# A vision-Mamba chain: the image convolution of three layers divided over four engines

## The chip, the cores and the metric

The kernel runs on one core of one Trainium2 chip. The metric is the device time of the whole program in microseconds (us), as the median of repeated executions. TensorE, VectorE, ScalarE, GpSimd and SyncE appear in the profile as PE (with PEld for its weight loads), DVE, ACT, POOL and SP. All data is float32.

## The reference

Eight images of 64 x 64 positions and 96 channels pass through four layers. Each layer adds to `x` what a selective-scan block makes of the group-normalized `x`. Cut to what matters here (layer 0; layers 1 and 2 differ in the order in which positions are walked, layer 3 has one direction and a causal convolution of three taps in its place):

```python
xz = gn(x) @ in_proj_w.T                      # 96 channels -> 2 * 192
xpart, z = split(xz, 2)
xc = depthwise_conv_3x3(xpart, conv_w)        # 192 channels, 9 taps each, SAME padding
xc = silu(xc + conv_b)
xs = [xc by rows, xc by columns, both reversed]              # K = 4 directions
dts, Bs, Cs = split(einsum(xs, x_proj_w))
delta = softplus(einsum(dts, dt_proj_w) + dt_proj_b)
for t in positions:                           # for each channel and 16 states
    h = exp(delta[t] * A) * h + delta[t] * u[t] * B[t]
    y[t] = sum_over_states(h * C[t])
y = layernorm(sum over directions of (y + D * u)) * silu(z)
x = x + y @ out_proj_w.T
```

## The kernel before

**Loops.** A hardware loop runs over the eight images. In its body the four layers stand one after the other, and within a layer the stages follow each other: normalization, convolution, scans, output. The 192 inner channels are held as a half 0 of 128 partitions and a half 1 of 64; the 4096 positions are eight chunks of 512, that is of eight image rows.

**Normalization.** DVE takes the statistics (L211), ACT forms `scale` with Ln and Exp (L227, L228), DVE forms `shift` (L230) and writes the normalized image `xn` with a border of zeros, chunk by chunk (L247).

**Convolution (L248 to L317).** The input projection and the nine taps are folded into one set of weights: `taps` is the tap times the projection (L197), and PE sums nine matmuls over shifted views of `xn` into one PSUM tile (L270). This makes 12 units: eight chunks of half 0, and four pairs of chunks of half 1, whose two chunks share one tile of 128 partitions. ACT applies SiLU with the bias (L290; L283 and L286 in layer 1, where even and odd columns go to different places) and a DMA stores the rows as `u_mem[0]` (L291, L297). The column order `u_mem[1]` is made by strided copies of DVE and GpSimd (L312 to L315) and stored (L316). In this stage the order on each engine is chosen by the framework's scheduler.

**Scans (`scans`).** 32 chunks are walked (eight in layer 3), 24 scan steps each. This part's order is written out by hand: a `plan` says in which of the 24 slots of a chunk each preparing step of the next chunk is issued, on PE, DVE, ACT and POOL in order. The steps that the text names:

- `scan` (L664, DVE): one recurrence of 128 x 512; its decay is made by `decay` four steps ahead (L650, ACT, Exp, six buffers), its input by `enter` (L633, PE, two PSUM buffers).
- `turn_v` (L521, PE) makes the delta projection and the B columns; `keep_b` (L551, ACT) keeps the latter.
- `softplus` (ACT): Abs (L542), Exp (L544), Ln (L546), twice a chunk, followed by `delta_of` (L556, DVE), `turn_back` (L607, PE) and `keep_delta` (L612, L616, ACT). The Ln of the first half stands in slot 6, that of the second in slot 13.
- `neg_a` (L764 on ACT, L765 on DVE) is made once a layer, before the first scan.
- `diagonal` (L577, POOL) and `diagonals` (L590, ACT) spread B; `keep` (L678, ACT) keeps states; `read_out` (L682, POOL) multiplies by C; `add_up` (L696, PE) sums over states; `close_sums` (L718 to L724, DVE) adds to the outputs.

**Activation tables.** Exp, Ln and SiLU need tables loaded into ACT. The kernel names the set itself, once for a stage, through `tables` (L108 to L112), and asks that the stage's instructions on ACT be issued after that load:

```python
load = tc.keep_in_program_order(tc.nc.scalar.preload_act_table_set(name))
with tc.issue_after(load.ins):
    yield
```

The convolution's set is `silu_and_others`; that of normalization and scans is `natural_log_exp_and_others`. Where the order that results leaves ACT with a set that lacks the next function, the build puts a load in front of that instruction.

Of the kernel before, what the change touches and what calls it, by code (L numbers as in the profile page):

```python
# [22 lines left out]
F32 = mybir.dt.float32  # L23
AF = mybir.ActivationFunctionType
ALU = mybir.AluOpType
# [3 lines left out]
NB, H, W, C = 8, 64, 64, 96  # L29
L = H * W  # L30
DI = 192
# [4 lines left out]
CH = 512  # L36
NCH = L // CH
# [8 lines left out]
class Layer:  # L46


    def __init__(self, dirs, rank, order, taps, norm):
        self.dirs, self.rank, self.order, self.taps, self.norm = dirs, rank, order, taps, norm  # L50

        self.x_rows = 33 + rank if dirs == 1 else 64 + 33 + rank
        at = 0
        for name, n in (
            ("win_x", DI),
            ("win_z", DI),
            ("x_proj", min(dirs, 2) * 2 * self.x_rows),
            ("dt_w", dirs * (DI + NS)),
            ("a_log", dirs * NT * NJ),
            ("d", dirs * 2),  # L60
            ("conv_b", 2),
            ("gamma", 2),
            ("beta", 2),
            ("w_out", 2 * C),
        ):
            setattr(self, name, at)
            at += n
        self.width = at
# [38 lines left out]
@contextmanager  # L107
def tables(tc, name):  # L108
# [55 lines left out]
def layer(tc, env, x, x_of, x_to, n, ly):  # L164

    nc = tc.nc
    const, small, big = env.const, env.small, env.big
# [6 lines left out]
    def mm(name):  # L174
        return env.ps_m.tile([128, CH], F32, tag="mm", name=name)
# [8 lines left out]
    def piece(name):  # L184
# [2 lines left out]

    w = env.wts.tile([128, W_MAX], F32, tag="w", name=f"w{n}")[:, : ly.width]
    nc.sync.dma_start(w, env.packs[n])
    taps = env.cpool.tile([C, 9 * DI], F32, tag="c", name=f"taps{n}")  # L190
    taps = taps[:, : ly.taps * DI].rearrange("p (t d) -> p t d", d=DI)
    nc.sync.dma_start(
        taps.rearrange("p t d -> p (t d)"), env.convs[n].partition_broadcast(C)
    )
# [30 lines left out]
    scale = small.tile([C, 1], F32, name="scale")  # L225
# [4 lines left out]
    nc.vector.scalar_tensor_tensor(shift, mean, -1.0, scale, ALU.mult, ALU.mult)  # L230


    image = ly.taps == 9
# [7 lines left out]
    for c in range(NCH):  # L241
        if image:
            to = xn[:, 1 + 8 * c : 9 + 8 * c, 1 : W + 1]
            of = chunk(c).rearrange("p (h w) -> p h w", w=W)
        else:
            to, of = xn[:, 2 + c * CH : 2 + (c + 1) * CH], chunk(c)
        nc.vector.tensor_scalar(to, of, scale, shift, ALU.mult, ALU.add)  # L247
    u_mem = [env.dram.tile([DI, L], F32, tag=f"u{o}", name=f"u{o}_{n}") for o in range(min(K, 2))]  # L248
    serpentine = ly.order == "serpentine"
    with tables(tc, "silu_and_others"):  # L250
        for half, (d0, nd) in enumerate(((0, 128), (128, 64))):

            u0 = [env.hpool.tile([128, L // 2], F32, tag="h", name="u0") for _ in range(2)]
            rows = [
                u0[c // 4][0:nd, c % 4 * CH : c % 4 * CH + CH].rearrange("p (h w) -> p h w", w=W)
                for c in range(NCH)
            ]

            for c0 in range(NCH if half == 0 else NCH // 2):
                both = (c0,) if half == 0 else (c0, c0 + NCH // 2)  # L260
                p = mm("conv")
                parts = [p[64 * o : 64 * o + nd] for o in range(len(both))]
                for t in range(ly.taps):
                    for c, part in zip(both, parts):
                        if image:
                            rhs = xn[:, 8 * c + t // 3 : 8 * c + t // 3 + 8, t % 3 : t % 3 + W]
                            out = part.rearrange("p (h w) -> p h w", w=W)
                        else:
                            rhs, out = xn[:, c * CH + t : (c + 1) * CH + t], part
                        nc.tensor.matmul(  # L270
                            out,
                            taps[:, t, d0 : d0 + nd],
                            rhs,
                            start=t == 0,
                            stop=t == ly.taps - 1,
                        )
                for o, (c, part) in enumerate(zip(both, parts)):
                    bias = w[64 * o : 64 * o + nd, ly.conv_b + half : ly.conv_b + half + 1]
                    got = part.rearrange("p (h w) -> p h w", w=W)
                    if serpentine:  # L280

                        even, odd = slice(0, W, 2), slice(1, W, 2)
                        nc.scalar.activation(  # L283
                            rows[c][:, :, even], got[:, :, even], AF.Silu, bias=bias
                        )
                        nc.scalar.activation(  # L286
                            rows[NCH - 1 - c][:, ::-1, odd], got[:, :, odd], AF.Silu, bias=bias
                        )
                    else:
                        nc.scalar.activation(rows[c], got, AF.Silu, bias=bias)  # L290
                        nc.sync.dma_start(  # L291
                            u_mem[0][d0 : d0 + nd, c * CH : (c + 1) * CH],
                            rows[c].rearrange("p h w -> p (h w)"),
                        )
            if serpentine:
                for r in range(2):
                    nc.sync.dma_start(  # L297
                        u_mem[0][d0 : d0 + nd, r * L // 2 : (r + 1) * L // 2], u0[r][0:nd]
                    )
            if K > 1:  # L300
                for v in range(2):
                    u1 = env.diags.tile([128, L // 2], F32, tag="diag", name="u1")
                    to = u1[0:nd].rearrange("p (w h) -> p w h", h=H)
                    for r in range(2):
                        of = u0[r][0:nd].rearrange("p (h w) -> p w h", w=W)
                        engine = nc.vector if r == 0 else nc.gpsimd
                        here = slice(32 * v, 32 * v + 32)
                        if serpentine:

                            there = slice(63 - 32 * v, 31 - 32 * v if v == 0 else None, -1)  # L310
                            up, down = slice(32 * r, 32 * r + 32, 2), slice(32 * r + 1, 32 * r + 32, 2)
                            engine.tensor_copy(to[:, :, up], of[:, here, 0::2])  # L312
                            engine.tensor_copy(to[:, :, down], of[:, there, 1::2])
                        else:
                            engine.tensor_copy(to[:, :, 32 * r : 32 * r + 32], of[:, here, :])  # L315
                    nc.sync.dma_start(  # L316
                        u_mem[1][d0 : d0 + nd, v * L // 2 : (v + 1) * L // 2], u1[0:nd]  # L317
                    )


    y_a = big.tile([128, L], F32, tag="big0", name="y_a")
# [3 lines left out]


    chunks = [slice(c * CH, (c + 1) * CH) for c in range(NCH)]
    halves = [slice(0, 64), slice(64, 128)]

    def single(o, name):  # L330
        return env.ps_y.tile([128, CH], F32, tag=f"y{o}", name=name)
# [474 lines left out]
    return a  # L806


def pack(ly, win, conv_b, x_proj, dt_w, dt_b, a_log, d, w_out, gamma=None, beta=None):
    K, R = ly.dirs, ly.rank  # L810
    XP = 33 + R
    a = np.zeros((128, ly.width), np.float32)
# [21 lines left out]
    d = d.reshape(K, DI)  # L834
    a[:, ly.d : ly.d + K] = d[:, :128].T
    a[0:64, ly.d + K : ly.d + 2 * K] = d[:, 128:].T
    for v, at in ((conv_b, ly.conv_b), (gamma, ly.gamma), (beta, ly.beta)):
# [17 lines left out]
def layouts(inputs):  # L855
    arrays = {"x": inputs["x"].reshape(-1, L, C).transpose(0, 2, 1), "const": constants()}
    for n, (ly, (pre, names)) in enumerate(zip(LAYERS, _NAMES)):
        arrays[f"pack{n}"] = pack(ly, *(inputs[pre + s] for s in names.split()))
# [23 lines left out]
```

## Time and profile before

| | |
|---|---|
| median of 3 runs | 33116.64 us (33102.38 to 33124.26) |
| profiled execution, its own time | 33112.82 us |
| its span in the profile | 33108.9 us |
| granted TensorE clock | 0.979 |
| DVE, ACT and POOL busy | 27562.6, 25739.6, 26418.0 us |
| folded-tap matmuls of the convolutions (L270) | 2580.0 us |
| table loads on ACT (L110) | 152, 1283 ns each |

Durations of single instructions come from the profiled execution. In a row of the profile, "out<-in" gives the tiles' names and "xcount | busy, mean ns of one | idle" how often, for how long, how long one takes, and how long its engine had stood idle before it. Instructions of one engine overlap a little, so the distance between the starts of two is less than the duration of one.

### The profile page before, as it was taken

The page shows a single profiled execution, that of the slowest core. Times are in us where ns is not written, and L with a number is a line of the kernel's source. Part 1 is how long each engine was busy: PE and PEld are TensorE (multiplying, and loading weights), DVE is VectorE, ACT ScalarE, POOL GpSimd, SP SyncE. Part 2 cuts the span into 40 slices and gives each one's busy share as a digit, 9 for nine tenths or more (in the row PEclk, how much of TensorE's full clock was granted, in tenths as well). Part 3 has the DMA queues.
Part 4 walks back from the last instruction along what each step waited for, and adds up shares of the span by engine and source line. Part 5 has one row for each costly group of instructions (what it writes and reads, how often), then busy time and mean ns, then how long its engine had stood idle before and what let it go on. Part 6 is the DMA issues. An engine that isn't in the chain of part 4 may idle for free.

```text
span 33108.9 us, 958242 instructions
## 1 busy us (share of the span) xinstructions
PE 32013.2 (97%) x406784; PEld 17321.5 (52%) x406784; DVE 27562.6 (83%) x28224; ACT 25739.6 (78%) x65112; POOL 26418.0 (80%) x8764
## 2 busy tenths in 40 slices
PE   9999999999999999999999999999999999999999
PEld 5555555555555555555555555555555455555555
DVE  8798887988879788798887988879888798887988
ACT  7787777877778777787777877778777787777877
POOL 7797777977779777797777977779777797777977
PEclk9999999999999999999999999999999999999999
DMA  3333333333333333333333333333333333333333
GB/s 84 73 77 80 72 83 73 77 79 72 83 73 78 78 72 84 73 78 78 72 84 73 78 78 72 84 74 77 79 72 84 73 77 78 73 83 74 77 79 72
DMA packets 1232983, 2550.36 MB, mean 77 GB/s; under 512 B 107024, under 2 KB 107024, under 8 KB 1202576
## 3 DMA queue, kind: packets, MB, share of 16 engines
q1 hardware_dynamic: 1228688, 2488.70, 33.6%
q8 instruction: 3232, 52.95, 0.7%
q14 instruction: 1063, 8.71, 0.1%
HBM read 2213.81 MB, written 274.46 MB: 75 GB/s over the span
## 4 chain that ended last, share of the span: by engine, by line


## 5 line engine op out<-in xcount | busy, mean ns | idle before, releaser
L682 POOL TENSOR_TENSOR h<-h,c 128x2048 f32<-128x2048 f32 x4992 | 22716.7, 4555 | 1984.7 <-ACT state L678 923.6
L664 DVE TENSOR_TENSOR_SCAN h<-d_a,state,dbu 128x512 f32<-128x512 f32 x17472 | 21080.0, 1261 | 1142.5 <-PE dbu L633 614.3
L650 ACT ACTIVATE d_a<-delta,neg_a 128x512 f32<-128x512 f32 x19968 | 14188.8, 716 | 45.2 <-DVE h L664 22.6
L633 PE MATMUL dbu<-diag,du_t 64*64 64x128 f32 x319488 | 11176.7, 277 | 228.8 <-DVE h L664 134.0
L633 PEld LDWEIGHTS dbu<-diag,du_t 64*64 64x64 f32 x319488 | 8746.7, 134 | 5025.0 <-issue 4641.1
L696 PE MATMUL y_ps<-h,const 128*64 128x512 f32 x39936 | 10805.5, 617 | 77.8 <-POOL h L682 64.8
L590 ACT ACTIVATE diag<-const,bt 128x64 f32<-128x64 f32 x26624 | 7840.9, 344 | 23.2 <-DMA u<-u 17.0
L577 POOL TENSOR_TENSOR diag<-const,bt 128x512 f32<-128x512 f32 x3328 | 3471.1, 1044 | 547.7 <-ACT bt L551 448.4
L664 DVE TENSOR_TENSOR_SCAN h<-d_a,dbu 128x512 f32<-128x512 f32 x2496 | 2893.4, 1204 | 437.8 <-PE dbu L633 238.2
L696 PEld LDWEIGHTS y_ps<-h,const 128*64 128x64 f32 x39936 | 2061.2, 135 | 1848.2 <-issue 1507.3
L521 PE MATMUL v<-w,x_dbl 39*128 39x208 f32 (+1 forms) x6656 | 2657.7, 483 | 159.5 <-ACT x_dbl L483 103.0
L521 PEld LDWEIGHTS v<-w,x_dbl 39*128 39x128 f32 (+1 forms) x6656 | 1796.9, 317 | 1736.9 <-issue 887.3
L270 PE MATMUL conv<-xn,taps 96*128 96x512 f32 (+1 forms) x7680 | 2580.0, 606 | 115.1 <-issue 69.6
L607 PEld LDWEIGHTS delta_ps<-const,delta_t 128*64 128x64 f32 (+1 forms) x19968 | 1678.8, 158 | 1422.6 <-issue 926.3
L616 ACT COPY delta<-delta_ps 64x512 f32<-64x512 f32 x3328 | 1930.5, 580 | 542.8 <-PE delta_ps L607 496.8
L607 PE MATMUL delta_ps<-const,delta_t 128*64 128x128 f32 (+1 forms) x19968 | 2277.6, 292 | 29.2 <-DVE delta_t L556 29.2
L270 PEld LDWEIGHTS conv<-xn,taps 96*128 96x128 f32 (+1 forms) x7680 | 1029.9, 167 | 1639.7 <-issue 1639.7
L551 ACT COPY bt<-v 128x32 f32<-128x32 f32 x1664 | 303.8, 183 | 1961.1 <-PE v L521 1960.5
L315 POOL COPY u<-u 128x1024 f32<-128x1024 f32 (+1 forms) x64 | 139.9, 2212 | 1736.3 <-ACT u L290 1736.3
L290 ACT ACTIVATE u<-conv,w 128x512 f32<-128x512 f32 (+1 forms) x384 | 263.2, 685 | 1619.1 <-PE conv L270 1481.5
L534 PEld LDWEIGHTS u_t<-const,u 128*128 128x128 f32 x3328 | 650.1, 195 | 1602.7 <-issue 887.6
L678 ACT COPY state<-h 128x4 f32<-128x4 f32 x4992 | 972.2, 195 | 546.5 <-DVE h L664 505.9
(86 smaller groups left out, 15802.0 us busy)
## 6 DMA issues: line engine op xcount, KB each, us to landing
c<-cm SPq DMA_DIRECT2D x1792, 512.0 KB
c<-xm SPq DMA_DIRECT2D x1536, 512.0 KB
u<-u SPq DMA_DIRECT2D x1024, 256.0 KB
u<-u SPq DMA_DIRECT2D x1024, 128.0 KB
u<-u SPq DMA_DIRECT2D x64, 1024.0 KB
x_mem<-x SPq DMA_DIRECT2D x48, 768.0 KB
x<-x_mem SPq DMA_DIRECT2D x48, 768.0 KB
u<-u SPq DMA_DIRECT2D x64, 512.0 KB
```

The costliest lines, as they stand in the source:

```text
L270: nc.tensor.matmul(out, taps[:, t, d0 : d0 + nd], rhs, start=t == 0, stop=t == ly.taps - 1,)
L521: nc.tensor.matmul(turned[i, e, "v"][:, b], block(2 * e + b, dbls[i]), w[0:XP, at : at + DI + NS], start=True, stop=True,)
L577: nc.gpsimd.tensor_tensor(diags[i, 0][:, b], sel.unsqueeze(1).unsqueeze(3).to_broadcast([128, NH, 64, 2]), of.unsqueeze(2).to_broadcast([1 ...
L590: nc.scalar.activation(diags[i, 1][:, b, q // 2, :, q % 2], sel, AF.Copy, scale=turned[i, b // 2, "b"][:, b % 2, NJ + q : NJ + q + 1],)
L607: nc.tensor.matmul(block(b, to), of_, ident, start=True, stop=True)
L616: nc.scalar.copy(delta[64 * half : 64 * half + 64], of)
L633: nc.tensor.matmul(to[64 * half : 64 * half + 64, e, b], du[rows, b, 64 * t : 64 * t + 64], diag[rows, b, 2 * half + pair], start=True, st ...
L650: nc.scalar.activation(d_a, deltas[i, t], AF.Exp, scale=neg_a[:, at : at + 1])
L664: nc.vector.tensor_tensor_scan(hs[s][:, m4, flow], decays.pop(m)[:, flow], p[:, flow], 0.0 if first else states[i // NCH][:, j : j + 1], A ...
L678: nc.scalar.copy(states[i // NCH][:, at : at + NH], hs[s][:, :, last])
L682: nc.gpsimd.tensor_tensor(hs[s], hs[s], cs[i, g], ALU.mult)
L696: nc.tensor.matmul(sums[i][o][64 * half : 64 * half + 64], sel, hs[of][:, state, :], start=g == 0 and e in (0, 4), stop=g == 1 and e in (3 ...
```

## The change

In layers 0 to 2 the convolution is divided. PE folds taps for four of the 12 units alone (chunks 4 to 7 of half 0). For the other eight units PE makes only the input projection (`project`), ACT copies it from PSUM into a bordered tile `xin` (`keep`), and nine scaled, shifted views of `xin` are summed (`by_sums`): on DVE for five units (all four pairs of half 1, and chunk 3 of half 0) into a PSUM tile, and for three units (chunks 0 to 2 of half 0) by ACT, which scales each view, and GpSimd, which adds it. The weight pack gains the taps as columns, and only the 128 folded columns of half 0 are made in layers 0 to 2. Column copies and row stores of both halves now stand after the convolution, half 1 first. Layer 3 keeps the folded form.

The core of the diff (the bodies that only moved into the functions `activate`, `by_taps`, `by_columns`, `by_rows` are left out):

```diff
...
     win_x = w[0:C, ly.win_x : ly.win_x + DI]
     nc.vector.tensor_tensor(
-        taps, taps, win_x.unsqueeze(1).to_broadcast([C, ly.taps, DI]), ALU.mult
+        taps, taps, win_x[:, 0:by_pe].unsqueeze(1).to_broadcast([C, ly.taps, by_pe]), ALU.mult
     )
...
     with tables(tc, "silu_and_others"):
-        for half, (d0, nd) in enumerate(((0, 128), (128, 64))):
...
-            for c0 in range(NCH if half == 0 else NCH // 2):
-                both = (c0,) if half == 0 else (c0, c0 + NCH // 2)
-                p = mm("conv")
...
+        if not image:
+            for c in range(NCH):
+                by_taps(0, (c,))
+            for c in range(NCH // 2):
+                by_taps(1, (c, c + NCH // 2))
+        else:
+            xin = big.tile([128, 2, 34, W + 2], F32, tag="big1", name="xin")
+            nc.gpsimd.memset(xin[:, :, :, 0 :: W + 1], 0.0)
...
+            def project(half, rows_):
+                n_, p = len(rows_[0]), wide("xin")[:, 0:CH]
+                d0, nd = widths[half]
+                for o, r in enumerate(rows_):
+                    nc.tensor.matmul(
+                        as_rows(p[64 * o : 64 * o + nd, 0 : n_ * W]),
+                        win_x[:, d0 : d0 + nd],
+                        xn[:, r[0] + 1 : r[0] + 1 + n_, 1 : W + 1],
+                        start=True,
+                        stop=True,
+                    )
+                return as_rows(p[:, 0 : n_ * W])
+
+            def keep(half, c, p):
+                nc.scalar.copy(xin[:, half, 1 + 8 * c : 9 + 8 * c, 1 : W + 1], p)
+
+            def by_sums(half, c, acc, together=True):
+                for t in range(9):
+                    of = xin[:, half, 8 * c + t // 3 : 8 * c + t // 3 + 8, t % 3 : t % 3 + W]
+                    at = ly.conv_w + 9 * half + t
+                    tap = w[:, at : at + 1]
+                    if not together:
+                        by = acc if t == 0 else piece("by_tap")
+                        nc.scalar.activation(as_rows(by), of, AF.Copy, scale=tap)
+                        if t:
+                            nc.gpsimd.tensor_tensor(acc, acc, by, ALU.add)
+                    elif t == 0:
+                        nc.vector.tensor_scalar(as_rows(acc), of, tap, None, ALU.mult)
+                    else:
+                        nc.vector.scalar_tensor_tensor(
+                            as_rows(acc), of, tap, as_rows(acc), ALU.mult, ALU.add
+                        )
+
+            edge = project(1, (range(32, 33), range(31, 32)))
+            nc.scalar.copy(xin[0:64, 1, 33:34, 1 : W + 1], edge[0:64])
+            nc.scalar.copy(xin[64:128, 1, 0:1, 1 : W + 1], edge[64:128])
+            nc.scalar.copy(xin[:, 0, 33:34, 1 : W + 1], project(0, (range(32, 33),)))
+            for c in range(4):
+                keep(1, c, project(1, (range(8 * c, 8 * c + 8), range(32 + 8 * c, 40 + 8 * c))))
+                keep(0, c, project(0, (range(8 * c, 8 * c + 8),)))
+            for c in range(4):
+                if c < 3:
+                    acc_p = env.decays.tile([128, CH], F32, tag="d_a", name="acc_p")
+                    by_sums(0, c, acc_p, False)
+                    activate(0, c, acc_p)
+                acc = single(c % 2, "acc")
+                by_sums(1, c, acc)
+                for o in range(2):
+                    activate(1, c + 4 * o, acc, o)
+                by_taps(0, (c + 4,))
+            acc = single(0, "acc")
+            by_sums(0, 3, acc)
+            activate(0, 3, acc)
+        for half in (1, 0):
             if serpentine:
-                for r in range(2):
-                    nc.sync.dma_start(
...
+                by_rows(half)
             if K > 1:
...
+                by_columns(half)
```

More of the change, by code (lines that the diff above doesn't have):

```diff
@@ L249, in layer @@
     serpentine = ly.order == "serpentine"
-    with tables(tc, "silu_and_others"):
-        for half, (d0, nd) in enumerate(((0, 128), (128, 64))):
[L253 to L257, printed above, removed]
-            for c0 in range(NCH if half == 0 else NCH // 2):
-                both = (c0,) if half == 0 else (c0, c0 + NCH // 2)
-                p = mm("conv")
[L262 to L275, printed above, removed]
-                        )
[L277 to L294, printed above, removed]
@@ new lines, in by_taps @@
+    def by_taps(half, both):
+        d0, nd = widths[half]
+        p = mm("conv")
+        for t in range(ly.taps):
+            for o, c in enumerate(both):
+                part = p[64 * o : 64 * o + nd]
+                if image:
+                    rhs = xn[:, 8 * c + t // 3 : 8 * c + t // 3 + 8, t % 3 : t % 3 + W]
+                    part = as_rows(part)
+                else:
+                    rhs = xn[:, c * CH + t : (c + 1) * CH + t]
+                nc.tensor.matmul(
+                    part, taps[:, t, d0 : d0 + nd], rhs, start=t == 0, stop=t == ly.taps - 1
+                )
+        for o, c in enumerate(both):
+            activate(half, c, p, o)
@@ new lines, in by_columns @@
+    def by_columns(half):
+        d0, nd = widths[half]
+        for v in range(2):
+            u1 = env.diags.tile([128, L // 2], F32, tag="diag", name="u1")
+            to = u1[0:nd].rearrange("p (w h) -> p w h", h=H)
+            for r in range(2):
+                of = u0[half][r][0:nd].rearrange("p (h w) -> p w h", w=W)
+                engine = nc.vector if r == 0 else nc.gpsimd
+                here = slice(32 * v, 32 * v + 32)
+                if serpentine:
+                    there = slice(63 - 32 * v, 31 - 32 * v if v == 0 else None, -1)
+                    up, down = slice(32 * r, 32 * r + 32, 2), slice(32 * r + 1, 32 * r + 32, 2)
+                    engine.tensor_copy(to[:, :, up], of[:, here, 0::2])
+                    engine.tensor_copy(to[:, :, down], of[:, there, 1::2])
+                else:
+                    engine.tensor_copy(to[:, :, 32 * r : 32 * r + 32], of[:, here, :])
+            nc.sync.dma_start(
+                u_mem[1][d0 : d0 + nd, v * L // 2 : (v + 1) * L // 2], u1[0:nd]
+            )
@@ L836, in pack @@
     a[0:64, ly.d + K : ly.d + 2 * K] = d[:, 128:].T
+    conv_w = conv_w.reshape(DI, ly.taps)
+    a[:, ly.conv_w : ly.conv_w + ly.taps] = conv_w[:128]
+    for p in (0, 64):
+        a[p : p + 64, ly.conv_w + ly.taps : ly.conv_w + 2 * ly.taps] = conv_w[128:]
     for v, at in ((conv_b, ly.conv_b), (gamma, ly.gamma), (beta, ly.beta)):
@@ L857, in layouts @@
     for n, (ly, (pre, names)) in enumerate(zip(LAYERS, _NAMES)):
-        arrays[f"pack{n}"] = pack(ly, *(inputs[pre + s] for s in names.split()))
+        arrays[f"pack{n}"] = pack(
+            ly, inputs[pre + "conv_w"], *(inputs[pre + s] for s in names.split())
+        )
     for n, (ly, (pre, _)) in enumerate(zip(LAYERS, _NAMES)):
```

72 lines of the change are left out of this document (44 added, 28 removed).

## The prediction

> **What bounds the kernel now.** I read the page first, then the stretches of one image, then the waits of a scan stage, last the seams between the stages, in order of time. In a row of stretches the columns are length, then busy time (and instructions) of PE, PEld, DVE, ACT, POOL, the granted clock, the DMA share and GB/s.
>
> ```profile
> 4154.30:4251.90 97.60, 97.60 (x291) 38.97 (x292) 4.32 (x7) 10.92 (x16) 3.90 (x2) 0.97 0.19 66
> 4251.90:4267.40 15.50, 11.71 (x75) 8.18 (x73) 7.35 (x7) 12.00 (x32) 8.92 (x6) 0.67 0.67 149
> 4267.40:5327.60 1060.20, 1048.40 (x15070) 595.55 (x15070) 1000.13 (x954) 931.44 (x2395) 990.48 (x315) 0.99 0.37 80
> ```
>
> These are layer 0 of the second image: convolution, seam, scans. The convolution is PE alone: 97.6 us with the other engines nearly idle. In the scans all four work: PE 99%, DVE 94%, POOL 93%, ACT 88%. There are 24 convolutions (8 images x 3 layers), so 2342 us lie in the first kind of stretch, and 24 x 1060 in the third.
>
> ```profile
> 300.00:1100.00 800.00, 797.54 (x11533) 453.72 (x11531) 762.10 (x729) 713.62 (x1840) 758.76 (x244) 1.00 0.37 81
> ...
> ACT bt L551 <- PE v L521: 55.7, 38, 1.8
> ACT delta L616 <- PE delta_ps L607: 18.6, 20, 1.2
> DVE h L664 <- PE dbu L633: 20.4, 28, 1.6
> ```
>
> Inside the scans of the first image, 800 us hold 24.3 chunks (146 `keep`, six a chunk), 32.9 us each. ACT works 29.4 us of a chunk and waits 3.55, nearly all of it for PE. PE sets the pace; ACT's spare is 3.55 us a chunk.
>
> ```profile
> L718 DVE SCALAR_TENSOR_TENSOR y_a<-u,d,y_ps 128x512 f32<-128x512 f32 x192 | 139.0, 724 | 31.5 <-PE y_ps L696 31.5
> L577 POOL TENSOR_TENSOR diag<-const,bt 128x512 f32<-128x512 f32 x3328 | 3471.1, 1044 | 547.7 <-ACT bt L551 448.4
> L765 DVE TENSOR_SCALAR neg_a<-neg_a 128x96 f32<-128x96 f32 x24 | 54.5, 2272 | 0.0
> L765 DVE TENSOR_SCALAR neg_a<-neg_a 128x24 f32<-128x24 f32 x8 | 1.4, 178 | 271.1 <-ACT neg_a L764 271.1
> L110 ACT ACT_TABLE_LOAD x152 | 195.0, 1283 | 77.2 <-PEq L144 73.6 <-PEq L869 1.1
> ...
> 2629.46 1.39 ACT L290 ACTIVATE u<-conv,w 64x512 f32<-64x512 f32 x2 [6.33 <-PE conv L270]
> 2630.87 1.28 ACT L110 ACT_TABLE_LOAD   x1
> 2632.16 0.28 ACT L764 ACTIVATE neg_a<-w 128x96 f32<-128x96 f32 x1
> ```
>
> The first two rows price a sum on DVE and an add on GpSimd. The last three show what a table load costs ACT: it starts 0.02 us after the last SiLU ended and the next instruction follows 0.01 us after it, 1.30 in all; the overlap of 0.10 that neighbours have (0.72 us decays start 0.62 apart) is lost too: **1.40 us**.
>
> **The convolution stage.** I count t from the end of `shift` (L230) in layer 2 of the first image, 2529.94; there PE begins at 2533.40 and the last SiLU ends at 2630.85, t = 100.9.
>
> - PE loses eight of 12 units of 7.72 us (nine matmuls of 0.858) and gains eight projections of 0.86: 36 x 0.858 + 8 x 0.86 = 37.8. It starts when `xn` chunk 4 is written: two chunks (0.98), 1152 of 1728 folded columns (1.30 of 1.95), three chunks (1.45), t = 3.7. The stretch's 96.0 us against 12 x 7.72 = 92.6 show 3.4 of slow start, which I keep; with the edges 0.5: PE ends at 45.4.
> - DVE gains 45 operations. The nearest row is L718, 0.724 with one PSUM input; dependent DVE operations start 0.03 after the one before: 40 x 0.754 + 5 x 0.54 (L247) = 32.9, from the first copied chunk at 8.5 to 41.4. Two column copies of half 1 stand between, 1.9 each as now beside GpSimd's (L315): 45.2. Bounds: 0.66 an operation (L724) and 1.26 (the scan, same shape), 41 to 65.
> - POOL gains 24 adds of 1.04 (L577; 1.14 as a quarter of L682): 25 us from t = 12, with two hand-overs from ACT of 2: 41.
> - ACT gains eight copies (0.49 apart, L616), three edges (0.25), 27 scalings (0.62 to 0.72) beside its 16 SiLU (0.70): 33 us from t = 4, with waits for all others.
>
> DVE's last sum is latest: its SiLU ends at 45.9. In the built order of layers 0 and 2, ACT then has this (in layer 1 the stage's own load comes after the last SiLU, as before):
>
> ```
> 47 L281 Activation u_166<-acc,w_118 128x512 [waits DVE_49]
> 48 L111 LoadActFuncSet
> 49 L281 LoadActFuncSet
> 50 L281 Activation u_167<-conv,w_118 128x512 [waits PE_49]
> 51 L850 LoadActFuncSet
> 52 L850 Activation neg_a_435<-w_118 128x96
> ```
>
> The last SiLU of a folded unit slipped behind the load of the scans' set. Two loads stand ahead of it: 45.9 + 2.6 + 0.7 = 49.2, **51.7 earlier** than 100.9. In layer 1 without them 46: 55.5 earlier than its 101.5.
>
> **The seam.** After row 51 the set in ACT is no longer the one with both Ln and Exp: the build loads in front of each Ln (L632) and of the first Exp after it. Up to the first decay that is five loads where one was: 4 x 1.30 = 5.2, of which the chain's waits for PE take about 1.2: +4 in layers 0 and 2, which gain 47.7. In layer 1 the first load of `u` waits for the row stores behind the last SiLU, now 2 MB of half 0 where 1 MB of half 1 was: 1 MB at the 178 GB/s of that seam is 6 us; layer 1 gains 49.5. The DVE and GpSimd copies of half 0 run after the last SiLU as those of half 1 did, 4 us. Sum: 16 x 47.7 + 8 x 49.5 = **1159 us saved**.
>
> The column copies and stores of half 0 moved behind the convolution. On SP's queue the two stores of 1 MB, which wait for the copies, stand ahead of the stores of `x_dbl` and the spreading of C, as the two of 0.5 MB of half 1 did; GpSimd's `diagonal` and DVE's `neg_a` stand behind the copies, again as before. The L765 rows show that neighbour: 2.27 us beside GpSimd's copies, 0.18 without. The 40 sums, which read PSUM as the scans do (1.26 us beside a GpSimd that is 93% busy), I leave free of it.
>
> **The scans.** Rows 48 to 52 go on: 64 pairs of loads in each scan stage of layers 0 and 2, four a chunk. The built program has 279 loads an image where 19 were: 2232 executed in place of 152. A chunk's ACT gains 4 x 1.40 = 5.6 us and has 3.55 to spare.
>
> What absorbs it: at slots 6 and 7 two loads put ACT 2.8 late; its wait of 1.76 for `turn_v` in slot 11 goes; at 13 and 14 two more; the wait of 0.9 for `turn_back` goes. What is left, about 2 us a chunk, eats the lead of three to four decays within two chunks; then DVE waits for decays and ACT sets the pace. Does ACT still wait then? DVE, held by ACT, finishes scan 9 before ACT is past decay 13, so PE has `turn_v` done 2 to 3 us before `keep_b`; `turn_back` comes out 2 us early as well. `delta_of` of slot 8 now waits for its Ln, about 1 us, which DVE (31.3 us a chunk) makes good by the chunk's end.
>
> So a scan stage is ACT's work: 933 us (931 to 936 in three layers) less 15 of the last chunk, plus 62 pairs x 2.8 = 174, makes 1092 for 31 chunks; plus 33 for the last, less the lead of 4: 1121, +61. I take +64 for small waits in the chunks that also copy `x_dbl`. The other end is all waits kept: +174. I take the low end since every input of ACT has slack. 16 x 64 = **1024 us lost**.
>
> The Trainium skill (ScalarE: Activation LUTs, What ACT_TABLE_LOAD costs) adds a drain of about 1380 ns to each switch of set. The trace shows none: 0.02 us before the load and 0.01 after. By the page a chunk's ACT would be some 40 us and the kernel about 2600 us slower (an estimate from its 2.66 us a switch). The same page (Table sets) says Exp and Ln share one set and need one load; that speaks against what the build makes of this change.
>
> **Sum.** 33112.8 (the profiled execution's own time, 3.8 under the median of 33116.6) - 1159 + 1024 = **32978 us**. About 0.2%, 66 us, is what a measurement can tell from no change.
>
> **The rivals.**
>
> 1. *ACT's waits stay (slower).* If PE or DVE is late for ACT somewhere in each chunk, half of the waits stay: +119 a layer, 1904 - 1159 = +745: 33858. It decides from 1159/16 = 72 a layer on, 0.37 us of waiting per chunk over the floor. For it: PE and DVE are over 90% busy even in the longer chunk, and buffers are two and six deep. Against: the slack of 2 us above. Chance 0.23.
> 2. *DVE's sums are long (slower).* At the scan's 1.26 us they end at t = 65, the saving falls by 20 in 24 layers, 480: 33458. For it: no row has PSUM both read and written. Against: L718 and L724 read PSUM at 0.66 to 0.72. Chance 0.15.
> 3. *The loads do not bite*, if ACT's spare covers them: the saving alone, 31954. Against: 5.6 is over 3.55. Chance 0.03.
>
> The forecast has 0.59: the saving off by 120, the loss between 57 and 80 a layer, its own range 32740 to 33350. Within it about 0.40 is faster by over 66, 0.13 within, 0.06 slower. With the rivals: faster 0.44, same 0.14, slower 0.42. The range of 32700 to 33850 leaves out the third rival, the slower half of the first and the forecast's edges.
>
> **What would show it.** Right: a convolution stretch of 46 to 49 us in place of 98; 2232 loads of 1.28; scan stages of layers 0 and 2 near 1124 with ACT at 99% and DVE waiting for decays and Ln; layer 1's scans unchanged at 1065. Wrong: `bt` still waiting for PE there, gaps around loads, or sums of over 0.8 us.

## The result, and the profile after

The changed kernel takes 33380.82 us (median, 33375.89 to 33389.05) against 33116.85 us before (the median above with a fourth run): ratio **1.008, 95% interval 1.0063 to 1.0098**. It is slower by 264 us where 139 us less were forecast; the time lies inside the stated range of 32700 to 33850. The profiled execution took 33389.05 us, its span 33383.4 us.

Cutting the span of each layer at five places (the first statistics, the end of `shift`, the last SiLU of the convolution, the first scan, the last scan) and adding the pieces up over eight images and four layers gives this ledger, in us:

| stage | before | after | difference | forecast |
|---|---|---|---|---|
| normalization | 586 | 594 | +8 | 0 |
| convolution | 2721 | 1971 | **-750** | **-1271** |
| seam | 620 | 717 | +97 | +112 |
| scans | 27502 | 28415 | +913 | +1024 |
| output | 1670 | 1677 | +7 | 0 |
| sum | 33099 | 33374 | +275 | -135 |

The forecast column is the prediction's own: 16 x 51.7 + 8 x 55.5, then 16 x 4 + 8 x 6, then 16 x 64. The scans were a little better than forecast; the convolution gained 521 us less, and that alone turns the sign.

Stretches of layers 0 and 1 of the second image after the change (columns as in the prediction): the convolution of layer 0, its seam, its scans, and the scans of layer 1. The last row lies inside the scans of the first image, as the 800 us shown of before.

```profile
4199.10:4263.40 64.30, 52.91 (x102) 18.71 (x101) 37.69 (x51) 34.95 (x55) 34.91 (x26) 0.77 0.29 80
4263.40:4283.80 20.40, 12.36 (x72) 8.88 (x72) 2.62 (x5) 16.34 (x35) 7.86 (x6) 0.50 0.80 228
4283.70:5394.20 1110.50, 1086.58 (x15070) 601.79 (x15070) 1006.63 (x954) 1092.55 (x2520) 989.35 (x315) 1.00 0.34 75
5570.10:6638.40 1068.30, 1053.07 (x15126) 598.27 (x15126) 1007.58 (x1077) 937.85 (x2418) 990.05 (x315) 0.99 0.37 79
...
300.00:1100.00 800.00, 788.52 (x10930) 436.89 (x10930) 727.27 (x693) 794.12 (x1833) 718.99 (x232) 1.00 0.35 78
```

In the scans of layer 0, ACT is busy 1092.55 of 1110.50 us, 98%: it has become the bound there, and layer 1, whose ACT has no extra loads, takes 1064 us on average where it took 1060. The convolution's row is 64.3 us long in place of 97.6 (it starts 0.9 us behind PE's first projection), and no engine fills it: PE 82%, DVE 59%, ACT and POOL 54%. The granted clock in it is 0.77. The seam is 20.4 us where the row of before had 15.5.

The rows of the new work (count, busy time, mean ns of one):

```profile
L632 ACT ACT_TABLE_LOAD x1024 | 1313.8, 1283 | 18.7
L736 ACT ACT_TABLE_LOAD x1008 | 1293.3, 1283 | 18.3
...
L381 DVE SCALAR_TENSOR_TENSOR acc<-xin,w,acc 128x512 f32<-128x512 f32 x960 | 690.2, 752 | 18.7
L377 POOL TENSOR_TENSOR acc_p<-acc_p,by_tap 128x512 f32<-128x512 f32 x576 | 728.4, 1266 | 847.8 <-ACT by_tap L375 483.2 <-issue 334.9
L379 DVE TENSOR_SCALAR acc<-xin,w 128x512 f32<-128x512 f32 x120 | 90.5, 754 | 554.2 <-ACT u L281 231.1 <-ACT u L277 184.6 <-ACT xin L365 138.6
```

The sums cost what was forecast, 752 ns for 754. GpSimd's adds cost 1266 ns where 1044 had been taken. The last row is the one that matters: at the first sums of its units DVE stood idle for 554.2 us, 23 us in each of 24 layers, and three quarters of it (231.1 + 184.6) was a wait for ACT's SiLU (L281; L277 in layer 1), which was in no term of the forecast.

That wait in the second image's layer 0, where `shift` ends at 4194.5. The columns are start, length, engine and operation; in brackets the idle time before it and who ended it. DVE, ACT and POOL, one after the other:

```profile
4208.34 8.78 DVE L381 SCALAR_TENSOR_TENSOR acc<-xin,w,acc 128x512 f32<-128x512 f32 x13
4226.28 0.75 DVE L379 TENSOR_SCALAR acc<-xin,w 128x512 f32<-128x512 f32 x1 [9.17 <-ACT u L281]
...
4244.77 0.75 DVE L379 TENSOR_SCALAR acc<-xin,w 128x512 f32<-128x512 f32 x1 [4.66 <-ACT u L281]
...
4250.71 1.05 DVE L322 COPY u<-u 64x1024 f32<-64x1024 f32 x1 [3.87 <-ACT u L281]
```

```profile
4224.25 0.72 ACT L281 ACTIVATE u<-acc_p,w 128x512 f32<-128x512 f32 x1 [0.95 <-POOL acc_p L377]
...
4249.25 0.72 ACT L281 ACTIVATE u<-acc_p,w 128x512 f32<-128x512 f32 x1 [4.51 <-POOL acc_p L377]
...
4259.44 0.69 ACT L281 ACTIVATE u<-acc,w 128x512 f32<-128x512 f32 x1 [7.48 <-DVE acc L381]
4260.15 1.28 ACT L111 ACT_TABLE_LOAD   x1
4261.44 1.28 ACT L281 ACT_TABLE_LOAD   x1
4262.73 0.69 ACT L281 ACTIVATE u<-conv,w 128x512 f32<-128x512 f32 x1
```

```profile
4238.54 10.67 POOL L377 TENSOR_TENSOR acc_p<-acc_p,by_tap 128x512 f32<-128x512 f32 x8 [2.06 <-ACT by_tap L375]
```

DVE had finished its first two units at 4217.1 and waited until 4226.3. Its sums alternate between two PSUM tiles, and a tile is free when its SiLU has read it. ACT works in order, and ahead of that SiLU stood the one at 4224.25, which waits for GpSimd's sum. The same happens at 4244.77, where ACT's scalings for GpSimd's third unit stand in the line as well. The column copy L322, which the scheduler put between two sums of the last unit, waits for SiLUs behind the one at 4249.25, and seven sums wait behind the copy and its neighbour. GpSimd's third round, the eight adds at 4238.54, ends at 4249.2. The last sum's SiLU comes at t = 64.9 instead of the forecast 45.2.

### The profile page after: what moved, and what is told of

The parts are those of the page before. It is cut to its first block, busy times and chain, and to the rows that moved or that the text cites. A ratio compares the mean times of both kernels' runs of the same rounds, so it can differ in the third digit from the quotient of the medians.

```text
span 33383.4 us, 954546 instructions
## 1 busy us (share of the span) xinstructions
PE 31673.9 (95%) x402320; PEld 17006.2 (51%) x402320; DVE 28358.1 (85%) x29304; ACT 28952.9 (87%) x68104; POOL 27140.7 (81%) x9436
## 3 DMA queue, kind: packets, MB, share of 16 engines
q1 hardware_dynamic: 1247120, 2483.64, 32.4%
## 5 line engine op out<-in xcount | busy, mean ns | idle before, releaser
L782 PE MATMUL y_ps<-h,const 128*64 128x512 f32 x39936 | 11483.3, 617 | 198.6 <-POOL h L768 180.6
L782 PEld LDWEIGHTS y_ps<-h,const 128*64 128x64 f32 x39936 | 2202.7, 135 | 2505.9 <-issue 1492.3
L557 PE MATMUL x_dbl<-u,w 64*103 64x512 f32 (+5 forms) x1792 | 1003.2, 644 | 442.6 <-DMA u<-u 250.6
L377 POOL TENSOR_TENSOR acc_p<-acc_p,by_tap 128x512 f32<-128x512 f32 x576 | 728.4, 1266 | 847.8 <-ACT by_tap L375 483.2
L642 DVE SCALAR_TENSOR_TENSOR delta_t<-v,rest 128x384 f32<-128x384 f32 x1664 | 897.2, 539 | 552.6 <-ACT rest L632 550.4
L632 ACT ACT_TABLE_LOAD x1024 | 1313.8, 1283 | 18.7
L736 ACT ACT_TABLE_LOAD x1008 | 1293.3, 1283 | 18.3
```

What stands on the lines that cost most here:

```text
L557: nc.tensor.matmul(dbls[i], w[0:n_, at : at + ly.x_rows], u[0:n_, half, :], start=half == 0, stop=half == 1)
L632: nc.scalar.activation(rests[i, e], rests[i, e], AF.Ln, bias=1.0)
L736: nc.scalar.activation(d_a, deltas[i, t], AF.Exp, scale=neg_a[:, at : at + 1])
L782: nc.tensor.matmul(sums[i][o][64 * half : 64 * half + 64], sel, hs[of][:, state, :], start=g == 0 and e in (0, 4), stop=g == 1 and e in (3 ...
```

## The experiments

Twelve kernels were run; e12 and e15 leave out part of the work. Their times and ledgers (stages as above, summed over the profiled execution; the ratio is to the kernel before, timed beside each):

| run | median us | ratio and interval | norm. | conv. | seam | scans |
|---|---|---|---|---|---|---|
| e1_pinned | 32353.56 | 0.9784 (0.9767 to 0.98) | 594 | 1949 | 661 | 27457 |
| e4_before_loads | 34041.81 | 1.0296 (1.0279 to 1.0313) | 588 | 2720 | 664 | 28375 |
| e3_pinned_acc | 32335.87 | 0.9779 (0.9763 to 0.9795) | 590 | 1895 | 685 | 27471 |
| e5_pinned_acc_proj | 32251.70 | 0.9752 (0.9735 to 0.9768) | 589 | 1822 | 706 | 27461 |
| e7_copies_last | 32256.62 | 0.9751 (0.9735 to 0.9767) | 589 | 1724 | 775 | 27470 |
| e10_two_gpsimd | 32164.02 | 0.972 (0.9704 to 0.9736) | 594 | 1633 | 764 | 27486 |
| e11_folded_first | 32267.54 | 0.9751 (0.9734 to 0.9767) | 598 | 1725 | 785 | 27494 |
| e12_no_gpsimd_sums | 32022.51 | 0.968 (0.9664 to 0.9697) | 584 | 1636 | 647 | 27454 |
| e13_warm | 32072.58 | 0.9695 (0.9679 to 0.9711) | 699 | 1453 | 767 | 27488 |
| e14_pinned_warm | 32240.84 | 0.9748 (0.9732 to 0.9765) | 696 | 1739 | 655 | 27460 |
| e15_no_gpsimd_sums_warm | 31872.26 | 0.9638 (0.9622 to 0.9654) | 690 | 1389 | 648 | 27474 |
| e16_warm_early | 31999.92 | 0.9675 (0.9662 to 0.9688) | 601 | 1459 | 759 | 27479 |

**The loads, taken away and put in alone.** In e1 the last SiLU is held in program order, so the folded unit's SiLU no longer slips behind the next stage's load, and each image is back to 19 loads. e4 is the kernel before with nothing but the loads.

```diff
# e1_pinned
-            activate(0, 3, acc)
+            activate(0, 3, acc, pin=tc.keep_in_program_order)   # around its nc.scalar.activation
# e4_before_loads: before, in the scans
-    with tables(tc, "natural_log_exp_and_others"):
+    with tables(tc, "exp_and_others" if n in (0, 2) else "natural_log_exp_and_others"):
```

> The changed kernel with one SiLU, the last of the convolution, pinned behind the one traced before it, so that no SiLU slips behind the load of the scans' set: 19 table loads an image instead of 279, the division of the convolution untouched. Theory (the loads set the pace of the scans of layers 0 and 2): scan stages back from 1110 and 1116 to 1060 us, seams 4 to 5 shorter, convolutions 2.6 shorter: 16 x 60 = 960 less than the changed kernel's 33381, 32420. Rival (the scans are slower for another reason that the division brings, and the loads are hidden): the scans stay above 1105 and the time falls by the seams and convolutions alone, 16 x 7 = 110, to 33270.

> The kernel before, its convolution untouched, with only the table loads added: the scans of layers 0 and 2 name a set that has Exp without Ln, so the build loads in front of each Ln and of the Exp after it, 275 loads an image. Theory (ACT paces the scans with its own work and its waits for PE vanish): +50 to +61 a scan stage and +5 a seam, 16 x 60 = 960: 34080. Rival (ACT's waits stay): +179 a layer, 35980. Rival (a drain of 1.38 us at each load): about +245 a layer, 37000.

e1 gave the scans back 958 us, and the ratio fell from 1.008 to 0.9784; e4 added 981 us to the kernel before. Its scans in layer 0 of the second image, with the loads and without the new convolution:

```profile
4392.10:5503.10 1111.00, 1087.02 (x15070) 601.66 (x15070) 1006.43 (x954) 1093.11 (x2521) 989.49 (x315) 1.00 0.32 76
...
L546 ACT ACT_TABLE_LOAD x1024 | 1313.8, 1283 | 18.3
L650 ACT ACT_TABLE_LOAD x1008 | 1293.3, 1283 | 17.9
```

ACT is busy 1093.11 of 1111 us, as in the changed kernel. The ledger's 873 us over 16 scan stages are 54.6 each, where the changed kernel lost 54.3 and 56.3. That the loads cost this in the scans, the forecast's boldest term, is confirmed from both sides; the size is 15% under its 64.

**The sums' buffers and the projections' buffers.** What remained was the convolution, 67.6, 71.6 and 68.0 us in layers 0 to 2 of e1. e3 gives the sums of two units buffers of their own; e5 adds to it that a pair of projections shares one wide buffer.

```diff
# e3_pinned_acc = e1 +
-                acc = single(c % 2, "acc")
+                acc = single(c, "acc") if c < 2 else wide("acc")[:, 0:CH]
# e5_pinned_acc_proj = e3 +
-                n_, p = len(rows_[0]), wide("xin")[:, 0:CH]
+                n_, p = len(rows_[0]), p[:, half * CH : half * CH + CH]   # p = wide("xin") once for each c
```

> The pinned kernel with the sums of the last two pairs of half 1 in two further PSUM buffers (free after the projections), so that DVE need not wait until ACT has read an old sum. Theory (DVE's 18 us of idling in the convolution is that wait, behind a SiLU that waits for GpSimd's sums): the last sum is no longer DVE's; the convolution ends with PE's folded units and GpSimd's sums, some 8 us earlier than in the pinned kernel, 24 x 8 = 190 less. Rival (DVE is held by late projections and nothing else): no gain, within 30 of the pinned kernel.

> In addition, a pair of half 1 and a chunk of half 0 are projected into the two halves of one PSUM buffer, so that four projections may be outstanding instead of two. Theory (PE runs at a clock of 0.50 for the 22 us of the projections because it waits for ACT's copies and so is never busy enough): the stretch shortens to 12 to 15 us, and the convolution by 6 to 8 more, 24 x 7 = 170 less than the run with more sum buffers. Rival (PE starts at half clock whatever it waits for): 2 to 3 a layer, 60 less.

Both came out near what the rivals had, -18 and -84 us. In e3 the waits of the first sums for a SiLU went, and one wait of 16.6 us at the column copy took their place; the end stayed tied to the SiLU behind GpSimd's last sum. In e5 the stretch of the projections still took 21.8 us in layer 0 of the second image, and the granted clock was at 0.50 for the first 19 of them.

**The column copy.** e7 holds that copy behind the last sum.

```diff
# e7_copies_last = e5 + the first VectorE copies of half 1 held in program order
-                by_columns(half)
+                by_columns(half, tc.keep_in_program_order if image and half == 1 else lambda ins: ins)
```

> This is e5_pinned_acc_proj (32251.7 us, ratio 0.9752) with VectorE's first column copies of the second half held behind the last sum. Theory (VectorE loses 16.1 us a layer at that copy, which the scheduler put between the sums of the last unit and which waits for SiLUs that stand in ScalarE's queue behind GpSimd's third sum): the last unit's sums run on before the copy, the last SiLU moves from about 6 us behind the SiLU of GpSimd's third sum to just behind it, and 24 layers save 4 to 6 us each: about 32130, ratio near 0.972. Rival (the copies are work that has to be done before the scans anyway, so what the convolution saves the seam gives back): within 30 us of e5, 32220 to 32260.

The rival came out. The convolution of layers 0 and 2 got 6 us shorter, the seam 4 to 5 us longer; layer 1 did not move. The copy now stands behind the sums and still waits for the same SiLU, until t = 55.5 (55.8 in e5):

```profile
4077.38 8.52 DVE L383 SCALAR_TENSOR_TENSOR acc<-xin,w,acc 128x512 f32<-128x512 f32 x12
4098.77 9.31 DVE L324 COPY u<-u 64x1024 f32<-64x1024 f32 x4 [12.86 <-ACT u L281]
```

**GpSimd's rounds.** e12 goes back to e1 and takes these rounds away; e10 gives one of the three units of GpSimd to VectorE.

```diff
# e12_no_gpsimd_sums = e1 +
-                for t in range(9):
+                for t in range(9 if together else 1):
# e10_two_gpsimd = e7 +
-                if c < 3:
+                if c < 2:
...
+            acc = single(1, "acc")
+            by_sums(0, 2, acc)
+            activate(0, 2, acc)
```

> e1_pinned (32353.6 us, ratio 0.9784) with the three units of ScalarE and GpSimd cut to their first tap: eight of their nine scalings and all of GpSimd's adds are left out, so the output lacks those taps. Theory (VectorE's waits in the convolution are for accumulators that ScalarE's SiLUs free, and these stand behind GpSimd's rounds): the three waits of 9.2, 4.7 and 3.9 us go, the stage ends about 11 us earlier a layer, with TensorE's last unit, and the time is near 32090, ratio 0.970. Rival (the late projections at half clock set VectorE's and TensorE's end, GpSimd's rounds only stand beside them): less than 3 us a layer, 32280 or above.

> e7_copies_last with two units by ScalarE and GpSimd in place of three, and six by VectorE in place of five. Theory (GpSimd's third round, 8 adds of 1.33 us and 2 us of hand-over, ends last): without it the stage ends with TensorE's last folded unit or VectorE's sixth sum (6 units of 6.8 us = 41 us from the first), 3 to 9 us earlier a layer than e7, so 70 to 220 us less. Rival (TensorE's four folded units, 36 us behind projections of 20 us at a granted clock of 0.50, end at the same time as GpSimd): under 40 us less than e7, or a few us a layer more where VectorE's sixth unit comes last.

Without GpSimd's rounds the convolutions of the three layers end 11.6, 15.3 and 12.0 us earlier than in e1, and the kernel is 331 us faster: the theory, at a somewhat higher price. Two of DVE's waits remain, shorter (5.0 and 2.5 us), and the stage now ends with PE's last folded unit:

```profile
4050.80 0.75 DVE L379 TENSOR_SCALAR acc<-xin,w 128x512 f32<-128x512 f32 x1 [5.05 <-ACT u L281]
...
4077.31 0.69 ACT L281 ACTIVATE u<-conv,w 128x512 f32<-128x512 f32 x1 [7.04 <-PE conv L299]
```

In e10 the kernel gains 93 us over e7, inside the theory's bounds.

**The clock.** In all these kernels the projections run at half clock (in e5, e7 and e10 all but their last 3 to 5 us). e11 puts one folded unit ahead of them; e13 (on e10), e14 (on e1) and e15 (on e12) add products that nobody reads while TensorE would idle.

```diff
# e11_folded_first = e10 + chunk 4's folded unit first
+            by_taps(0, (4,))        # ahead of the first project(), which is held behind it
...
-                by_taps(0, (c + 4,))
+                if c:
+                    by_taps(0, (c + 4,))
# e13, e14, e15: in the normalization, five ahead of m_ps and six behind v_ps
+    if image:
+        busy = wide("busy")
+        for _ in range(5):
+            tc.keep_in_program_order(nc.tensor.matmul(
+                busy[0:C, 0:CH], groups, chunk(NCH - 1), start=True, stop=True
+            ))
...
```

> e10_two_gpsimd with the first folded unit (18 half-length or 9 full matrix products) put ahead of the projections. Theory (the half clock comes from TensorE's interrupted start: in the kernel before, where folded taps follow each other without gaps, the granted clock was full 4 to 5 us into the stage): the projections behind it run at a granted clock near 1.0 and take about half their time, and TensorE ends 5 to 9 us earlier a layer, 100 to 200 us less in all unless VectorE's later start takes it back (first sum at about 14 us instead of 8.5). Rival (the clock stays near 0.50 until some 20 us into the stage whatever TensorE does first): no gain over e10, up to 120 us more from VectorE's later start.

> e10_two_gpsimd (32164 us, ratio 0.972) with eleven matrix products of the raw x added on TensorE around the group statistics, five before them and six between them and the projections; nothing reads what they write. Theory (the projections run at a granted clock of 0.50 because TensorE comes to them after some 20 us of idling, and their short bursts do not lift it; e11, where a folded unit ran ahead, showed them at 1.00): the clock is full by about 3 us after the projections begin, their stretch takes 12 to 13 us in place of 21.5, TensorE's last unit and VectorE's sums end 6 to 9 us earlier a layer, 24 layers save 150 to 210 us: about 31980, ratio 0.967. Rival (the projections fall back to 0.50 by themselves, or wait for ScalarE's copies at the same pace): within 40 us of e10.

> e1_pinned (32353.6 us, ratio 0.9784) with the same eleven matrix products. Theory (GpSimd's three rounds hold VectorE's and TensorE's buffers and set the end, whatever the projections do): GpSimd's first add comes a few us earlier with the quicker projections, and the stage ends 2 to 5 us earlier a layer, 50 to 120 us less: about 32270, ratio 0.976. Rival (the half clock is the main cause of the stage's 18 us over the forecast): 9 us or more a layer, 32140 or below.

> e12_no_gpsimd_sums (32022.5 us, ratio 0.968; eight of the nine taps of the three units of ScalarE and GpSimd left out) with the same eleven matrix products. Theory (with GpSimd's rounds out of the way, TensorE's projections at half clock are what is left of the difference to the forecast's 46 to 49 us): the last SiLU comes at 47 to 50 us in place of 56, 24 layers save 145 to 215 us: about 31840, ratio 0.9625. Rival (something else ends the stage, VectorE's sums held by the two sum buffers): under 3 us a layer, 31950 or above.

e11's theory was right on the clock and wrong on the time: the projections took 12.8 us (4070.8 to 4083.6) in place of 21.9, but DVE's first sum came at t = 18.2 instead of 9.2, and PE's last unit then waited for a SiLU that stood behind GpSimd's second sum. It is 103 us slower than e10. (The 4 to 5 us that its theory gives for the kernel before are too short: there the clock was full 10 us behind `shift`, 6 after PE's first matmul.)

```profile
4070.81 2.60 PE L357 MATMUL xin<-xn,w 96*64 96x64 f32 x10
...
4083.60 12.18 PE L299 MATMUL conv<-xn,taps 96*128 96x512 f32 x28
4102.50 10.25 PE L299 MATMUL conv<-xn,taps 96*128 96x512 f32 x18 [6.72 <-ACT u L281]
```

The clearest pair is e12 and e15, which differ only in the added products. The projections with three folded matmuls among them, then the rest of the stage; e12 first:

```profile
4026.90:4048.60 21.70, 21.70 (x36) 6.09 (x37) 12.97 (x20) 8.76 (x16) 0.00 (x0) 0.50 0.19 54
4048.60:4079.20 30.60, 30.57 (x71) 13.03 (x69) 23.09 (x31) 9.78 (x15) 5.91 (x3) 1.00 0.48 126
```

```profile
4017.70:4029.20 11.50, 11.50 (x38) 3.68 (x38) 8.04 (x12) 8.32 (x16) 0.00 (x0) 1.00 0.21 61
4029.20:4059.00 29.80, 29.80 (x71) 12.86 (x69) 26.05 (x37) 9.30 (x15) 5.34 (x3) 1.00 0.53 140
```

The same matmuls take 21.7 us at a granted clock of 0.50 and 11.5 us at 1.00. The convolutions of e15 take 45.7, 46.0 and 45.7 us, 10.3 less than e12's, where its theory had 6 to 9; DVE's wait of 5.0 us is gone too. Its total, 150 us less than e12, is inside the theory's bounds because the normalization took 106 us back. e14's total, -113 us, is in its theory's bounds, but for a mixed reason: the convolution gained 8.3 to 9.0 us a layer, close to what the rival asked for, and the normalization lost 4 to 5, because `m_ps` stood behind the added products in PE's queue. e13 fell short of its theory for that reason: 180 us gained in the convolution, 105 lost in the normalization.

e16 mends that: four products of the half of `x` that lands first, and four behind the statistics.

> e13_warm (32072.6 us, ratio 0.9695) with eight added matrix products in place of eleven: four of the first half of x, which lands some 3 us before the second, ahead of the group statistics, and four behind them. Theory (the eleven keep the group statistics waiting in TensorE's queue, 4 to 5 us a layer in the stretch from the first statistics to `shift`, which took half of what the clock brought): that stretch returns to within 1 us of e10's 8.4, 21.6 and 21.6, the convolution keeps e13's 46 to 48, and 24 layers save 70 to 110 us: about 31985, ratio 0.967. Rival (eight are too few to lift the clock to full before the projections): the convolution goes back towards e10's 54, 32070 to 32160.

The normalization is back at 601 us and the convolution stays at 1459, as its theory said. But eight products are not always enough: in three of the 24 layers the clock was at 0.50 through most of the projections, and these convolutions took 6 to 7 us longer. Layer 1 of the second and of the third image, 15 us from about 4.5 us behind `shift`:

```profile
5213.00:5228.00 15.00, 15.00 (x24) 4.62 (x23) 9.71 (x16) 5.95 (x12) 3.79 (x3) 0.54 0.00 1
9215.90:9230.90 15.00, 15.00 (x41) 5.45 (x40) 12.92 (x21) 11.61 (x21) 8.03 (x7) 1.00 0.01 1
```

With the eleven products of e13, e14 and e15 the projections ran at 1.00 in every layer. With 32000 us and a ratio of 0.9675 e16 is the fastest of the kernels that compute everything, against 1.008 for the change as made.

## Why the prediction was wrong

**The step that failed** is the end of the convolution stage: "DVE's last sum is latest: its SiLU ends at 45.9", and from it 51.7 and 55.5 us saved. Measured: 69.0, 71.7 and 69.3 us in the three layers, so 32.4, 29.8 and 31.8 saved; 8 x (19.3 + 25.7 + 19.9) is 519 us, the ledger's missing 521 but for rounding. Two causes, shown by the four kernels e1, e12, e14 and e15:

| convolution in layers 0, 1, 2 | clock as it comes | clock raised |
|---|---|---|
| with GpSimd's rounds | 67.6, 71.6, 68.0 (e1) | 59.3, 62.6, 59.3 (e14) |
| without them | 56.0, 56.3, 56.1 (e12) | 45.7, 46.0, 45.7 (e15) |

Two limits of the table: in e14 and e15 the added products also hold PE, so that its first projection comes at t = 4.4 and not 3.7, and the 1.35 us in which DVE folds the weights fall into the longer normalization; and e12 and e15 lack ACT's scalings along with GpSimd's adds, so that the two are not told apart. The forecast without the two loads in layers 0 and 2 was 46.6 (49.2 - 2.6), and 46 in layer 1. With both causes away the stage takes 45.7 to 46.0, so nothing else of size is missing. That is not the forecast come true engine by engine: PE ends last, at t = 44.4 at full clock from its start, where the forecast's 45.4 held 3.4 us of slow start; DVE's last sum ends at 43.2 instead of 45.2; and the forecast's terms for GpSimd and ACT are not tested there.

- *The clock.* The prediction copied the slow start of before, 3.4 us, and priced a projection at 0.86, as a matmul of the folded taps at full clock. In the changed kernel the clock did not rise within the projections:

```profile
4198.20:4220.00 21.80, 21.75 (x36) 6.11 (x37) 13.03 (x20) 9.15 (x17) 6.70 (x6) 0.50 0.00 0
4220.00:4250.00 30.00, 29.85 (x67) 12.80 (x65) 15.08 (x21) 20.25 (x33) 23.65 (x19) 0.95 0.31 89
```

  Before, in the same layer, the folded taps had lifted it (here `shift` ends at 4150.3):

```profile
4155.34:4160.34 5.00, 5.00 (x7) 1.92 (x6) 0.64 (x2) 0.00 (x0) 0.00 (x0) 0.50 0.00 0
4160.34:4165.34 5.00, 5.00 (x13) 2.34 (x12) 0.00 (x0) 0.00 (x0) 0.00 (x0) 0.97 0.00 0
```

  By the clock records of the two traces this holds throughout: the clock rose 8 to 11 us behind `shift` in all 24 layers before, and 27 to 31 us behind it after. PE ended its units at t = 55.3, not 45.4. Worth 8.3 to 9.0 us a layer with GpSimd's rounds, 10.3 to 10.4 without. The Trainium skill (TensorE: Matmul & The Clock Gate, What's actually happening) says that about 3.4 us of sustained activity lift the clock from half to full. The two rows of before are of that order, though longer (0.97 from t = 10 on, PE having begun at about 4: some 6 us); the 21.8 us of after, in which the records show PE busy throughout, are not, and the measurement decides. The ends of matmuls are modelled in the records, so PE may have paused where they show it busy; that this is the reason was not shown.

- *Waits in line.* The prediction gave each engine its work and took the latest end. It asked what is queued behind the copies and in the scans, but not what ACT's SiLUs for DVE and PE are queued behind: GpSimd's sums. Those were also mis-sized: an add of 128x512 took 1.27 us (1.33 between starts) where L577's 1.04 was taken, though the quarter of L682, 1.14, stood beside it; 24 x 0.29 is 7 us. Even at full clock (e14) the third round ends at t = 46.5 in place of 41. Rounds and the waits behind them are worth 11.6 to 15.3 us a layer (13.6 to 16.6 at full clock), shown by e12 and e15, which also leave out ACT's scalings for them. The column copies took some 6 us of the stage in layers 0 and 2, and e7 only moved most of that into the seam.

**Right:** the 2232 loads (1024 + 1008 + 152 + 48 at three other lines), 1283 ns each; that ACT comes to pace the scans, though the loss, 54.3 and 56.3 us a stage, is under the 64 that was taken, and under the low end of 61 and the range of 57 to 80 as well; the seam, +4.0 and +2.4 (forecast +4) and +5.6 in layer 1 (+6); the sums' 0.754; layer 1's scans, 1064 (1065). The two L765 rows that were to show GpSimd's copies as a bad neighbour compare 96 columns with 24, but the reading holds: in e1, without the neighbour, the 96 columns took 0.20 us. Not as described: in the scans DVE's waits were to be for decays and Ln. They are put down mostly to PE's `dbu` and POOL's to ACT's states, in the 800 us shown above:

```profile
DVE h L750 <- PE dbu L719: 59.6, 70, 2.3
POOL h L768 <- ACT state L764: 52.2, 33, 2.3
...
DVE delta_t L642 <- ACT rest L632: 8.1, 14, 0.8
```

ACT paces (794.12 of 800 us), but the delay reaches the others through what stands behind ACT, not at ACT's own decays; the wait of `bt` for PE, 55.7 us before, is gone, as the low end of the price demanded.

The Trainium skill's rule that the prediction weighed against the trace (ScalarE: Activation LUTs, What ACT_TABLE_LOAD costs): its 1283 ns is what the rows show; its drain of about 1380 ns after each switch is not in these rows (a load starts 0.02 us after the SiLU before it, and what follows 0.01 us after its end). e4 adds 2048 loads over the kernel before and 981 us, 0.48 us each, since part fell into ACT's spare.

**The rivals.** None came as described. Rival 1 (ACT's waits stay) and rival 3 (loads don't bite) are refuted by e4. Rival 2 had the right place, a convolution that ends at t = 65, and the wrong mechanism: the sums are not long, they wait. That the 480 us it was priced at come near the 521 that were missing is luck.

## What to carry to other kernels

When work is divided over engines, add up not only each engine's work but the queue of the engine that drains all of them: a reader that works in order ties the fast producers' buffers to the slowest producer. Price TensorE's matmuls by the clock in the row that they will stand in, not by the row that they come from; here, eight to eleven products that nobody reads, ahead of a stretch of short bursts, were worth 6 to 10 us a layer of convolution, if they do not stand in front of work that is waited for. And look at what an edit does to the order around a table load: holding one SiLU in place took the ratio from 1.008 to 0.9784, more than all else that was tried here together.

## What the hardware showed that was not expected

- The granted clock stayed at 0.50 through 21.8 us of projections (three folded matmuls among them) that follow an idle stretch, and at 1.00 through the projections when eleven products (e13 to e15) or one folded unit (e11) ran ahead of them; with eight (e16) it did so in 21 of 24 layers. What in the projections keeps it low was not settled.
- GpSimd's add of two 128x512 tiles took 1266 ns, where its product with a spread input had shown 1044.
- Two table loads in a row cost 1.28 us each with 0.01 us between them (4260.15 and 4261.44 above).
